# A transformer stack on one core: the order of loads, mask checks and value projections at the head of the first attention

## The chip, the core and the metric

The kernel is one program for one NeuronCore of a Trainium2 chip. TensorE (PE in the profile) multiplies matrices, VectorE (DVE), ScalarE (ACT) and GpSimd (POOL) do the rest, and SyncE (SP) issues most of the transfers. Each engine has a queue of its own, which it works off strictly in order; engines wait for each other by semaphores. The metric is the time of one execution on the device in microseconds (us).

## The reference, cut to what matters

Input are 2048 tokens `x` of width 256, a context of 1601 rows of width 256, and two integer masks of 2048 x 1601. Four layers follow, each a cross attention and a feed-forward block with a residual sum around each. Only the first attention and the masks matter here:

```python
x = x + L0_xattn(layernorm(x), ctx, Wq, Wk, Wv, Wo, bo)   # 8 heads of 64, no mask
# q = xn @ Wq, k = ctx @ Wk, v = ctx @ Wv, weights = (256, 512)
# out = softmax(q k^T / 8) v, then @ Wo + bo
```

The masks are used by later attentions only. The kernel has two versions of everything behind the first feed-forward block: a short one for masks of a certain pattern, and a general one. Which of them runs is decided by a look at all of both masks, and that look is done beside the first attention.

## The kernel before, in words

**Start.** `Net.__init__` issues 16 loads of `x`, one for each 128 tokens, on SP (L70). `load_context` issues 13 loads of context rows on ACT's queue (L123), transposes them on PE (L130) and copies the result into `ctxT` on ACT (L135). `attention0` then issues the four weights on SP (L313): keys, values, queries, output.

**Projections.** For each of four pairs of heads and four pieces of the context (512, 512, 512 and 65 columns) PE computes the keys (L338); ACT copies them in fp32 (`kT`, L342) and VectorE casts them to bf16 (`kb`, L343). Then PE computes the values for 13 tiles of context rows (L348), copied to `v` by VectorE for odd tiles (L353) and by ACT for even ones (L355). All these results pass through the same three PSUM banks (`pm`).

**Units.** The attention is worked in 16 units: 4 chunks of 512 tokens times 4 pairs of heads. `prepare` makes what a unit needs: the normalized tokens (once for each chunk), the queries (L367; copies L371 and L372), and the maximum of each row of scores. The maxima come from bf16 products, two heads side by side (L380), of which VectorE takes a maximum each (L385: 24 for each unit, then L396 and L400), and they are turned by PE (L406) into the shift `sh` (L407). The unit itself goes over 13 tiles of context rows, two tiles to a group `g`: `scores` (L458, L460 on PE, then the exponential on ACT, L465, into one of five buffers `p0`), and for the group before, `values` (L472 on PE; the sum of the exponentials on POOL, L479 and L481). Between these steps the generator of the next unit's `prepare` (`nxt`) and of the last unit's `finish` (`done`) are advanced by single steps. `finish` makes one product (L414), copies it (L418), takes four reciprocals on VectorE (L422) and multiplies (L424). Unit 0 has no predecessor, and so no `finish`; its own `prepare` runs ahead of it as a whole (L442).

**The looks at the masks.** `look_at_masks` is a generator. It loads 128 rows of a mask in two transfers, the first 1201 columns (`head`, L276) and the last 400 (`tail`, L278); ACT squares and adds up the head (L291), VectorE compares the tail with the first row of the mask (`mrow`, L293) and counts. There are 16 such looks for each mask, 32 in all, with two buffers. `attention0` advances the generator once at the end of unit 0 and then twice in each unit (L494).

**What sets the order.** In the first attention only PE's queue follows the source (L441, `manual_schedule`). The queues of ACT, VectorE, POOL and SP are ordered by a planner. It has put all 32 looks ahead of or into unit 0: on ACT the first comes behind four copies of keys, on VectorE the last one (L293, then L298 and L299) comes in the middle of unit 0.

Of the kernel before, what the change touches and what calls it, by code (L numbers as in the profile page):

```python
# [8 lines left out]
F32 = mybir.dt.float32  # L9
# [3 lines left out]
ALU = mybir.AluOpType  # L13
AX = mybir.AxisListType

P = 128
# [38 lines left out]
class Net:  # L55


    def __init__(self, ctx, tc, a, out):
        self.tc, self.nc, self.a, self.out = tc, tc.nc, a, out
        nc = self.nc  # L60
        self.const = ctx.enter_context(tc.tile_pool(name="const", bufs=1))
        self.small = ctx.enter_context(tc.tile_pool(name="small", bufs=4))
        self.wraw = ctx.enter_context(tc.tile_pool(name="wraw", bufs=3))
        self.xnp = ctx.enter_context(tc.tile_pool(name="xnp", bufs=2))


        self.x = []
        for t in range(NT):
            xt = self.const.tile([P, D], F32, name=f"x{t}")
            nc.sync.dma_start(xt, a["x"][0, t * P : (t + 1) * P, :])  # L70
            self.x.append(xt)

        self.ident = self.const.tile([P, P], F32, name="ident")
        make_identity(nc, self.ident)
        self.identb = self.const.tile([P, P], BF16, name="identb")
        make_identity(nc, self.identb)
        self.ones = self.const.tile([P, P], F32, name="ones")
        nc.vector.memset(self.ones, 1.0)
        self.negones = self.const.tile([1, P], BF16, name="negones")
        nc.vector.memset(self.negones, -1.0)  # L80
        self.mhalf = self.const.tile([P, TPC], F32, name="mhalf")
        nc.vector.memset(self.mhalf, -0.5)
        self.phalf = self.const.tile([P, TPC], F32, name="phalf")
        nc.vector.memset(self.phalf, 0.5)
        self.mone = self.const.tile([P, TPC], F32, name="mone")
        nc.vector.memset(self.mone, -1.0)

        self.ready = 0
        self.ctxT = self.const.tile([P, 2, NCTX], F32, name="ctxT")
# [161 lines left out]
    def look_at_masks(self, pool, names):  # L251

        nc = self.nc
        odd = pool.tile([P, len(names) * (2 * NT + 1)], F32, name="odd", bufs=1)
        self.rows = {}
        col = 0

        def flag():  # L260
            nonlocal col
            col += 1
            return odd[:, col - 1 : col]

        todo, loaded = [], []
        for k, n in enumerate(names):
            m = self.a[n].rearrange("b s k -> (b s) k") if n.startswith("mask_B") else self.a[n].rearrange("a b s k -> (a b s) k")
            row = self.const.tile([P, NTAIL], mybir.dt.int32, name=f"mrow{k}")
            nc.sync.dma_start(row, m[0, K0:].partition_broadcast(P))
            self.rows[n] = row  # L270
            todo += [(m, t, row) for t in range(NT)]

        def load():
            m, t, row = todo.pop(0)
            head = pool.tile([P, K0], mybir.dt.int32, name="head")
            nc.sync.dma_start(head, m[t * P : (t + 1) * P, :K0])  # L276
            tail = pool.tile([P, NTAIL], mybir.dt.int32, name="tail")
            nc.sync.dma_start(tail, m[t * P : (t + 1) * P, K0:])  # L278
            loaded.append((head, tail, row))

        for _ in range(2):
            load()
        yield
        for n in names:
            seen = self.small.tile([P, 1], F32, name="seen")
            junk = pool.tile([P, NTAIL], BF16, name="junk", bufs=1)
            nc.vector.tensor_scalar(junk, self.rows[n], 0.0, 0.0, ALU.not_equal, ALU.add, accum_out=seen)
            nc.vector.tensor_scalar(flag(), seen, 0.0, None, ALU.is_equal)
        while loaded:
            head, tail, row = loaded.pop(0)  # L290
            nc.scalar.activation(head, head, AF.Square, accum_out=flag())  # L291
            junk = pool.tile([P, NTAIL], BF16, name="junk", bufs=1)
            nc.vector.scalar_tensor_tensor(junk, tail, 1.0, row, ALU.mult, ALU.not_equal, accum_out=flag())  # L293
            if todo:
                load()
            yield
        self.some = self.const.tile([P, 1], F32, name="some")
        nc.vector.tensor_reduce(self.some, odd, AX.X, ALU.add)  # L298
        nc.vector.tensor_scalar(self.some, self.some, 0.0, None, ALU.is_gt)  # L299


    def attention0(self, look):

        tc, nc, a = self.tc, self.nc, self.a
        H, DH = 8, 64
        HP = H // 2
        halves = [slice(0, DH), slice(DH, P)]
        wk, wv = (x.rearrange("p (k f) -> p k f", k=2) for x in self.weights("kv0", 1024, 1024))
        wq, wo = self.weights("qo0", 1024, 1024)
        wq = wq.rearrange("p (k f) -> p k f", k=2)  # L310
        wo = wo.rearrange("p (k f) -> p k f", k=4)
        for v, n in ((wk, "Wk"), (wv, "Wv"), (wq, "Wq"), (wo, "Wo")):
            nc.sync.dma_start(v, a[f"L0_xattn_{n}"].rearrange("(k p) f -> p k f", p=P))  # L313
        with ExitStack() as s:
            self.banks(s, m=3, a=1)
            kv = s.enter_context(tc.tile_pool(name="kv0", bufs=1))
# [17 lines left out]
            for hp in range(HP):  # L334
                for k0, n in PIECES:
# [5 lines left out]
                        )  # L341
                    nc.scalar.copy(kT[:, hp, k0 : k0 + n], ps[:, :n])  # L342
                    nc.vector.tensor_copy(kb[:, hp, k0 : k0 + n], ps[:, :n])  # L343
            for kt in range(NKT):
                r = rows_of(kt)
                ps = self.pm()
                for kc in range(2):
                    nc.tensor.matmul(  # L348
                        ps[:r, :], lhsT=self.ctxT[:, kc, kt * P : kt * P + r], rhs=wv[:, kc, :],
                        start=kc == 0, stop=kc == 1,  # L350
                    )
                if kt % 2:
                    nc.vector.tensor_copy(v[:r, kt, :], ps[:r, :])  # L353
                else:
                    nc.scalar.copy(v[:r, kt, :], ps[:r, :])  # L355

            xnTs = {}

            def prepare(c, hp, made):
# [78 lines left out]

            units = [(c, hp) for c in range(NCH) for hp in range(HP)]
            made = []  # L440
            s.enter_context(tc.manual_schedule(engines={mybir.EngineType.PE}))  # L441
            drain(prepare(*units[0], made))  # L442
            attn = done = None
            for u, (c, hp) in enumerate(units):
                nxt = prepare(*units[u + 1], made) if u + 1 < len(units) else None
# [39 lines left out]
                for g, kts in enumerate(groups):  # L485
# [5 lines left out]
                    for kt in late:  # L491
                        values(kt)
                    late = kts
                    if u and g in (3, 5):  # L494
                        step(look, 1)
                    if g:
                        step(nxt, 1)
# [1655 lines left out]
@with_exitstack  # L2153
def network(ctx: ExitStack, tc: tile.TileContext, a, out):
    net = Net(ctx, tc, a, out)
    net.load_context()
    masks = ("mask_BxSxS2_ik0", "mask_1x1xSxS2_ik0")
    with tc.tile_pool(name="look", bufs=2) as pool:
        net.attention0(net.look_at_masks(pool, masks))
    room = ctx.enter_context(tc.tile_pool(name="w1", bufs=1)).tile([P, 1536], F32, name="w1")  # L2160
    dram = ctx.enter_context(tc.tile_pool(name="e0d", bufs=1, space=bass.MemoryType.DRAM))
    odd, due, gates, raw = net.experts0(dram, ("L1_xattn", room))
# [67 lines left out]
```

## Time and profile before

| | |
|---|---|
| median of 3 runs | 1833.39 us (1827.76 to 1833.9) |
| the profiled execution | 1826.28 us, its span 1824.2 us |
| granted clock of TensorE, mean | 0.976 |
| PE busy | 1699.6 us of the span |
| first product of keys (L338) | at 19.97 us |
| first product of values (L348) | at 46.14 us |
| first scores of unit 0 (L458) | at 95.72 us |
| end of unit 0 (copy L505) | at 144.10 us |
| end of unit 1 (copy L505) | at 179.36 us |
| looks, head on ACT (L291) | 1.21 us each, and 0.19 us for reading the sum |
| looks, tail on VectorE (L293) | 0.56 to 2.59 us, median 0.58 us |

The profile covers one execution. Each digit of a row of engines is the busy share of 1/40 of the span in tenths, so each slice is 45.6 us. A line of the timeline gives the start, the time, the engine and the source line of a group of instructions, and in brackets how long the engine had been idle and what ended that. A line of the chain of waits gives start, time and what the end of the program had to wait for there. In a table of stretches, the columns after the time are the busy times of PE, the weight loads, VectorE, ACT and POOL with the number of instructions, then the granted clock, the busy share of the transfer engines, and GB/s.

### The profile page before, as it was taken

Reading aid. Unit: us, or ns where it says so; the run is one execution under the profiler, and the core shown is the slowest. Engines: PE = TensorE matmul, PEld = TensorE weight load, DVE = VectorE, ACT = ScalarE, POOL = GpSimd, SP = SyncE. Lnnn points to the kernel's source line nnn. Section 1 sums busy time; section 2 is a strip of 40 time slices with the busy share of each in tenths; the row PEclk is TensorE's granted clock in tenths of the full one; section 3 lists DMA queues with packets and bytes.
Section 4 is the critical chain, followed back from the end, with each engine's and each line's share of the span. In section 5 each row is a group of like instructions: output and inputs, shape, how many; then the busy total and the mean of one; then the engine's idle time right before and its main releaser. Section 6 shows DMA issues by size and latency. Waiting matters only on the chain.

```text
span 1824.2 us, 21267 instructions
## 1 busy us (share of the span) xinstructions
PE 1699.6 (93%) x8102; PEld 848.0 (46%) x8102; DVE 909.8 (50%) x1737; ACT 728.5 (40%) x963; POOL 690.8 (38%) x477
## 2 busy tenths in 40 slices
PE   6879999999999998999999999999988789999898
PEld 3323334333333334444457863664576622332687
DVE  4664565555664543662844643422045567786300
ACT  3554443453443442223234522111135456666222
POOL 2047886876887683002202730100026400211210
PEclk9889999999999998999999999999989889999999
DMA  8870000000000000454300010000000001010651
GB/s 271 280 229 1 1 1 1 1 1 1 1 1 1 1 0 12 163 220 173 111 13 1 1 32 1 1 1 0 0 1 1 13 13 21 17 22 13 221 184 39
DMA packets 52461, 94.11 MB, mean 52 GB/s; under 512 B 10093, under 2 KB 37374, under 8 KB 51454
## 3 DMA queue, kind: packets, MB, share of 16 engines
q1 hardware_dynamic: 49776, 88.92, 14.8%
q0 software_dynamic: 768, 2.10, 0.4%
q10 hardware_dynamic: 1806, 1.64, 0.3%
q8 instruction: 66, 1.08, 0.2%
q14 instruction: 45, 0.37, 0.1%
HBM read 69.30 MB, written 19.01 MB: 48 GB/s over the span
## 4 chain that ended last, share of the span: by engine, by line
PE 72%; DVE 12%; ACT 5%; DMA 4%; POOL 3%; issue 3%; SPq 0%; ACTq 0%; DVEq 0%; POOLq 0%
PE pa L472 8%; PE psc L460 6%; PE pa L557 6%; PE psc L1058 5%; PE pa L1078 5%; PE psc L1980 4%; DVE mp L385 4%; PE pa L2143 3%; PE psc L2132 3%; DVE ri L422 3%; PE pa L1449 2%; PE psc L458 2%; ACT p L1987 2%; PE pm L380 2%; PE pm L431 2%
## 5 line engine op out<-in xcount | busy, mean ns | idle before, releaser
L481 POOL TENSOR_TENSOR sp<-sp,p 128x1024 f32<-128x1024 f32 (+1 forms) x176 | 418.5, 2378 | 57.7 <-ACT p L465 47.0
L385 DVE TENSOR_REDUCE mp<-pm 128x1 f32<-128x512 f32 x384 | 242.8, 680 | 159.7 <-PE pm L380 159.0
L465 ACT ACTIVATE p<-psc 128x1024 f32<-128x1024 f32 (+1 forms) x208 | 212.9, 1024 | 260.5 <-PE psc L460 166.9
L460 PE MATMUL psc<-qT,kT 64*128 64x512 f32 (+1 forms) x832 | 221.6, 594 | 0.0
L472 PE MATMUL pa<-p,v 128*64 128x512 f32 (+1 forms) x832 | 202.3, 608 | 0.0
L1987 ACT ACTIVATE p<-psc 100x1024 f32<-100x1024 f32 x128 | 124.4, 1021 | 62.7 <-PE psc L1980 54.7
L1965 DVE TENSOR_REDUCE ms<-psc 128x2 bf16<-128x800 f32 x128 | 124.2, 988 | 46.0 <-PE psc L1961 43.4
L380 PE MATMUL pm<-kb,qb 64*128 64x512 bf16 x384 | 100.5, 389 | 27.5 <-DVE mp L385 26.0
L557 PE MATMUL pa<-w_e,xe 128*128 128x512 f32 x256 | 118.7, 614 | 0.0
L472 PEld LDWEIGHTS pa<-p,v 128*64 128x64 f32 (+1 forms) x832 | 50.9, 137 | 129.8 <-issue 126.8
L1058 PE MATMUL psc<-q,kT 128*128 128x512 f32 (+1 forms) x208 | 102.2, 610 | 0.0
L171 DVE TENSOR_SCALAR xn<-x,mv,rstd 128x256 f32<-128x256 f32 x128 | 58.2, 512 | 87.7 <-PE pm L185 52.2
L156 POOL TENSOR_SCALAR rstd<-mv 128x4 f32<-128x4 f32 x32 | 9.8, 308 | 228.6 <-DVE mv L152 185.2
L1078 PE MATMUL pa<-v,p 128*128 128x257 f32 (+1 forms) x416 | 95.3, 382 | 0.0
L460 PEld LDWEIGHTS psc<-qT,kT 64*128 64x128 f32 (+1 forms) x832 | 86.0, 185 | 19.5 <-issue 6.3
L1980 PE MATMUL psc<-q,kT 32*100 32x512 f32 x512 | 82.0, 653 | 13.2 <-ACT p L1987 11.5
L458 PE MATMUL psc<-sh,negz 64*128 64x512 bf16 (+1 forms) x416 | 87.7, 384 | 2.1 <-ACT sh L407 2.0
L1030 DVE TENSOR_REDUCE mp<-pm 128x1 f32<-128x512 f32 x64 | 34.4, 571 | 102.5 <-PE pm L1025 102.2
L1078 PEld LDWEIGHTS pa<-v,p 128*128 128x128 f32 (+1 forms) x416 | 77.5, 190 | 11.8 <-issue 0.2
L567 ACT COPY y<-pa 128x512 f32<-128x512 f32 x64 | 37.6, 587 | 96.6 <-PE pa L557 94.3
L557 PEld LDWEIGHTS pa<-w_e,xe 128*128 128x128 f32 x256 | 48.0, 194 | 55.6 <-issue 52.3
L479 POOL TENSOR_TENSOR sp<-p,p 128x1024 f32<-128x1024 f32 x16 | 37.7, 2354 | 89.4 <-ACT p L465 89.4
(376 smaller groups left out, 2730.2 us busy)
## 6 DMA issues: line engine op xcount, KB each, us to landing
table<-y SPq DMA_DIRECT2D x32, 512.0 KB, 3.2
w<-in_L_ffn_w_dram SPq DMA_DIRECT2D x16, 1024.0 KB, 6.2
head<-in_mask_BxSxS_ik_dram SPq DMA_DIRECT2D x16, 600.5 KB, 4.0
head<-in_mask_1x1xSxS_ik_dram SPq DMA_DIRECT2D x16, 600.5 KB, 4.0
bc<-turned SPq DMA_DIRECT2D x7, 1024.0 KB, 7.0
tail<-in_mask_BxSxS_ik_dram SPq DMA_DIRECT2D x16, 200.0 KB, 4.1
tail<-in_mask_1x1xSxS_ik_dram SPq DMA_DIRECT2D x16, 200.0 KB, 3.6
x<-in_x_dram SPq DMA_DIRECT2D x16, 128.0 KB, 4.0
```

What stands on the lines that cost most here:

```text
L380: nc.tensor.matmul(pair[j][:, :wd], lhsT=qb[h, i * P : (i + 1) * P], rhs=kb[h, hp, k0 : k0 + wd], start=True, stop=True,)
L385: nc.vector.tensor_reduce(mp[:, i, j, n : n + 1], pair[j][:, :wd], AX.X, ALU.max)
L460: nc.tensor.matmul(sc[:r, j, :], lhsT=kT[h, hp, kt * P : kt * P + r], rhs=q[h, :], start=False, stop=True,)
L465: nc.scalar.activation(p[:r], sc[:r], AF.Exp, scale=DH**-0.5)
L472: nc.tensor.matmul(acc[h, :], lhsT=v[:r, kt, hp * P + h.start : hp * P + h.stop], rhs=p[:r, j, :], start=kt == 0, stop=kt == NKT - 1,)
L481: nc.gpsimd.tensor_tensor(sums[:r], sums[:r], p[:r], ALU.add)
L557: nc.tensor.matmul(ps, lhsT=xnT[t // TPC][:, kc, (t % TPC) * P : (t % TPC + 1) * P], rhs=ew[kc][:, 2 * h : 2 * h + 2, :], start=kc == 0, s ...
L1058: nc.tensor.matmul(sc[:r, j, :], lhsT=kT[:, kc, ks], rhs=q[:, kc, :], start=kc == 0, stop=False)
L1078: nc.tensor.matmul(acc[:, : D + 1], lhsT=p[:r, kt, i * P : (i + 1) * P], rhs=v[:r, kt, :], start=kt == 0, stop=kt == NKT - 1,)
L1965: nc.vector.tensor_reduce(ms[u % 2][:, i, 64 * k + DH : 64 * k + 64 : 32], ps[:, :, :NTAIL], AX.X, ALU.max)
L1980: nc.tensor.matmul(sc[j // 2][:TR, j % 2, :], lhsT=kT[h, g, kt * TR : (kt + 1) * TR], rhs=q[u][h, :], start=True, stop=True,)
L1987: nc.scalar.activation(p[:TR], sc[k][:TR], AF.Exp, scale=DH**-0.5)
```

## The change

1. The weights of the keys are issued ahead of everything else on SP (`weights0`), then those of the values; the 16 loads of `x` come behind these two, and then the weights of queries and outputs.
2. A look loads its 1601 columns in one transfer, `both`; head and tail are views of it.
3. In the first attention ACT's queue follows the source too. Each look makes ACT copy one element per partition (`one`, from a tile of ones) behind its pass over the head, and VectorE's pass over the tail takes `one` as its factor in place of the constant 1.0, so it can't start before ACT's.
4. The generator of the looks is advanced three times in a unit, in groups 1, 3 and 5, instead of twice.
5. The 13 products of values are made between the steps of the first unit's `prepare`, instead of ahead of it.

In the generated order of after, VectorE's and SP's queues are still the planner's. All 32 looks then stand in units 1 to 11. In VectorE's queue of such a unit, the first look stands behind 4 of the 24 maxima; the second behind `finish`'s multiplication and 4 more maxima; the third behind the last maxima. Two small passes over the masks' first rows (L287, L288 of before) stay between the second and third cast of keys, and the statistics of all 16 tiles of `x` (L151) stay ahead of the first cast. Apart from looks, the queues of units 1 to 15 and of all that follows hold the same instructions in the same order.

```diff
         self.x = []
         for t in range(NT):
-            xt = self.const.tile([P, D], F32, name=f"x{t}")
-            nc.sync.dma_start(xt, a["x"][0, t * P : (t + 1) * P, :])
-            self.x.append(xt)
+            self.x.append(self.const.tile([P, D], F32, name=f"x{t}"))
...
         def load():
             m, t, row = todo.pop(0)
-            head = pool.tile([P, K0], mybir.dt.int32, name="head")
-            nc.sync.dma_start(head, m[t * P : (t + 1) * P, :K0])
-            tail = pool.tile([P, NTAIL], mybir.dt.int32, name="tail")
-            nc.sync.dma_start(tail, m[t * P : (t + 1) * P, K0:])
-            loaded.append((head, tail, row))
+            both = pool.tile([P, NCTX], mybir.dt.int32, name="both")
+            nc.sync.dma_start(both, m[t * P : (t + 1) * P, :])
+            loaded.append((both[:, :K0], both[:, K0:], row))
...
             nc.scalar.activation(head, head, AF.Square, accum_out=flag())
+
+            one = self.small.tile([P, 1], F32, name="one")
+            nc.scalar.copy(one, self.ones[:, 0:1])
             junk = pool.tile([P, NTAIL], BF16, name="junk", bufs=1)
-            nc.vector.scalar_tensor_tensor(junk, tail, 1.0, row, ALU.mult, ALU.not_equal, accum_out=flag())
+            nc.vector.scalar_tensor_tensor(junk, tail, one, row, ALU.mult, ALU.not_equal, accum_out=flag())
...
-    def attention0(self, look):
+    def weights0(self):
+        wkv = self.weights("kv0", 1024, 1024)
+        self.nc.sync.dma_start(
+            wkv[0].rearrange("p (k f) -> p k f", k=2), self.a["L0_xattn_Wk"].rearrange("(k p) f -> p k f", p=P)
+        )
+        return wkv
+
+    def attention0(self, look, wkv):
...
-        for v, n in ((wk, "Wk"), (wv, "Wv"), (wq, "Wq"), (wo, "Wo")):
+        for v, n in ((wv, "Wv"), (wq, "Wq"), (wo, "Wo")):
             nc.sync.dma_start(v, a[f"L0_xattn_{n}"].rearrange("(k p) f -> p k f", p=P))
+            if n == "Wv":
+                for t in range(NT):
+                    nc.sync.dma_start(self.x[t], a["x"][0, t * P : (t + 1) * P, :])
...
-            for kt in range(NKT):
...
-                    nc.scalar.copy(v[:r, kt, :], ps[:r, :])
...
-            s.enter_context(tc.manual_schedule(engines={mybir.EngineType.PE}))
-            drain(prepare(*units[0], made))
+            s.enter_context(tc.manual_schedule(engines={mybir.EngineType.PE, mybir.EngineType.Activation}))
+
+            first = prepare(*units[0], made)
+            for kt in range(NKT):
+                r = rows_of(kt)
+                ps = self.pm()
+                for kc in range(2):
+                    nc.tensor.matmul(
+                        ps[:r, :], lhsT=self.ctxT[:, kc, kt * P : kt * P + r], rhs=wv[:, kc, :],
+                        start=kc == 0, stop=kc == 1,
+                    )
+                if kt % 2:
+                    nc.vector.tensor_copy(v[:r, kt, :], ps[:r, :])
+                else:
+                    nc.scalar.copy(v[:r, kt, :], ps[:r, :])
+                if kt:
+                    step(first, 2 if kt > 1 else 1)
+            drain(first)
...
-                    if u and g in (3, 5):
+                    if u and g in (1, 3, 5):
                         step(look, 1)
...
     net = Net(ctx, tc, a, out)
+    wkv = net.weights0()
     net.load_context()
...
-        net.attention0(net.look_at_masks(pool, masks))
+        net.attention0(net.look_at_masks(pool, masks), wkv)
```

More of the change, by code (lines that the diff above doesn't have):

```diff
@@ L307, in attention0 @@
         halves = [slice(0, DH), slice(DH, P)]
-        wk, wv = (x.rearrange("p (k f) -> p k f", k=2) for x in self.weights("kv0", 1024, 1024))
+        wk, wv = (x.rearrange("p (k f) -> p k f", k=2) for x in wkv)
         wq, wo = self.weights("qo0", 1024, 1024)
@@ L343, in attention0 @@
                     nc.vector.tensor_copy(kb[:, hp, k0 : k0 + n], ps[:, :n])
-            for kt in range(NKT):
[L345 to L354, printed above, removed]
-                    nc.scalar.copy(v[:r, kt, :], ps[:r, :])
             xnTs = {}
```

## The prediction

> **What bounds the kernel now.** First the page, for the share of each engine and where in the span PE isn't full:
>
> ```profile
> PE 1699.6 (93%) x8102; PEld 848.0 (46%) x8102; DVE 909.8 (50%) x1737; ACT 728.5 (40%) x963; POOL 690.8 (38%) x477
> PE   6879999999999998999999999999988789999898
> DMA  8870000000000000454300010000000001010651
> ```
>
> PE is the bound, except in the first three slices (137 us), where the transfers are full. Then those slices stage by stage, in the table of stretches:
>
> ```profile
> 46.00:70.00 24.00, 22.84 (x56) 9.79 (x56) 9.18 (x24) 14.08 (x24) 0.00 (x0) 1.00 0.82 267
> 70.00:96.00 26.00, 16.74 (x51) 5.01 (x51) 20.45 (x41) 14.45 (x24) 3.31 (x4) 0.69 0.84 288
> 96.00:144.00 48.00, 39.47 (x172) 14.27 (x172) 30.06 (x57) 27.15 (x36) 27.55 (x12) 0.88 0.60 190
> 144.00:179.40 35.40, 34.12 (x178) 11.95 (x178) 19.87 (x32) 16.07 (x19) 28.55 (x13) 1.00 0.00 1
> ```
>
> Unit 0 (third row) takes 48 us, unit 1 only 35.4. What unit 0 waits for is in the chain of waits: mask transfers, each released by the look before it.
>
> ```profile
> 85.91 1.30 ACT head L291 x2
> 87.23 4.03 DMA head<-in_mask_1x1xSxS_ik_dram
> ...
> 115.83 3.52 DMA tail<-in_mask_1x1xSxS_ik_dram
> 119.44 2.21 DVE junk L293 x2
> ```
>
> Last the looks themselves, by tile, and then the timeline, POOL beside VectorE:
>
> ```profile
> L293 DVE SCALAR_TENSOR_TENSOR junk<-tail,mrow x32: 557/576/2591, 30.7 to 127.7; 128x400 bf16<-128x400 int32 x32
> ```
>
> ```profile
> 110.02 2.45 POOL L481 TENSOR_TENSOR sp<-sp,p 128x1024 f32<-128x1024 f32 x1 [0.18 <-ACT p L465]
> 118.86 5.00 POOL L481 TENSOR_TENSOR sp<-sp,p 128x1024 f32<-128x1024 f32 x2 [6.38 <-ACT p L465]
> 110.32 2.59 DVE L293 SCALAR_TENSOR_TENSOR junk<-tail,mrow 128x400 bf16<-128x400 int32 x1
> 119.44 2.21 DVE L293 SCALAR_TENSOR_TENSOR junk<-tail,mrow 128x400 bf16<-128x400 int32 x1 [0.62 <-DMA tail<-in_mask_1x1xSxS_ik_dram]
> ```
>
> The same look takes 0.56 us or four times that: the first slow one ends at 112.91, 0.44 after POOL's sum (110.02 + 2.45 = 112.47). The second gets in between two sums. Every slow look ends about 0.44 us behind a POOL sum.
>
> **The change, part by part.** It takes the looks out of the head and puts three into each of units 1 to 11. So two sums.
>
> *Keys.* L338 starts at 19.97, waiting for Wk, the 17th load on SP. Now Wk is first, 16 loads of `x` come later by two transfers, and the first normalization isn't needed before 45 us: hidden. ACT must first issue its 13 context loads (until 12.6) and load its table (1.28), so PE can start at 12.5 to 15. But VectorE's queue is next: 16 statistics, two casts, the two passes over `mrow`, then the other casts. The last statistic ended at 17.9; 1 MB of weights now goes ahead of `x`, at 0.27 MB/us 3.7 us: 21.5. Two casts: 23. `mrow` has the same bytes ahead of it on SP as before, so it lands as before: 18.31 + 7.3 = 25.6. Two passes (1.35): the third cast starts at 27.0, against 30.0. PE can run only three banks ahead; at 27.6 it has 8 large pieces (4 records of 0.43 = 1.72) and 3 small ones (0.22) left, 14.4: end 42.0, against 46.1. Bounds of this gain: 0 (`mrow` 4 us later) and 7.5 (no wait but PE's).
>
> *Values and the first maxima.* Before: 46.1 to 95.7, 49.6 us, of which PE's 52 records of values are 22.4 and VectorE's 24 maxima are 14.4 (16 took 9.55 from 80.5 on, 0.60 each), one after the other, with ACT's waits for masks between, and at half clock from 80 to 100. Now: three products of values, 8 transposes (1.0) and the queries (1.7): 7.9. Then six rounds of one product (1.72) and four maxima. The next product needs the bank of the second maximum, 1.6 us after the last product's end where ACT copies it, 2.0 where VectorE does: 6 x 3.55 = 21.3. Then four products, the last maxima and the turn: 8.3. Sum 37.5. Bounds: PE alone 28.5; nothing overlapped 43.5.
>
> *Unit 0.* 48.4 before. Unit 1's 35.3 less `finish`'s product (1.1) and PE's waits for the reciprocals (1.8): 32.4; PE alone 31.2, all of unit 1 35.3.
>
> End of unit 0: 42.0 + 37.5 + 32.4 = 111.9 against 144.1, gain 32. One stretch at half clock after the wait near 25 would cost 1.7: I take 31, from 25 to 36.
>
> *Looks in a steady unit.* ACT: 1.21 + 0.19 + the one-column copy, not in the trace; nearest is the reading of the sum, 0.19. Together 1.5 (the reading overlaps). It fits before the next exponential at all three places (gaps of 2.47, 2.97 and 2.04 us in unit 1), so ACT costs nothing; without that gap 1.6 each. Transfers: one of 0.8 MB in place of two is issued two looks, some 20 us, ahead, in units where nothing else is moved: nothing (a landing took 3.6 to 6.2). SP issues 32 instead of 64; past its first two mask loads go the two expert weights of 1 MB, the second waiting for the buffer of keys' and values' weights; the third mask load behind it isn't needed before unit 1. VectorE, by unit 1's timeline:
>
> ```profile
> 151.98 9.63 POOL L481 TENSOR_TENSOR sp<-sp,p 128x1024 f32<-128x1024 f32 x4
> 153.21 2.58 DVE L385 TENSOR_REDUCE mp<-pm 128x1 f32<-128x512 f32 x4 [0.92 <-PE pm L380]
> 162.26 5.05 POOL L481 TENSOR_TENSOR sp<-sp,p 128x1024 f32<-128x1024 f32 x2 [0.64 <-ACT p L465]
> 165.93 3.87 DVE L385 TENSOR_REDUCE mp<-pm 128x1 f32<-128x512 f32 x6 [0.86 <-PE pm L380]
> ```
>
> Look A (group 1) comes behind the exponential that ends at 151.88; with ACT's 1.5 and a semaphore it is released at 153.5, in the middle of a sum that ends at 151.98 + 2.41 = 154.4 (9.63 for four); with 0.44 and the reading (0.08) it ends at 154.95. The maxima behind it start 1.7 us late. Behind those are queued the bank for L414, its copy, the reciprocals, the multiplication and the next maxima, and PE waits for all of them in turn (the chain of waits runs over them from 153.2 to 163.3 in this unit). PE's maximum of 154.08 waits for a bank till 155.6, L414 moves from 154.64 to 156.2: PE loses 1.55. Look B (group 3), behind the exponential that ends at 164.1, is released at 165.7; the second of the two sums ends at 167.3, the look at 167.8; the maxima that started at 165.93 are 1.9 late, PE's next maximum needs a bank and PE loses 1.6. Look C finds VectorE idle: nothing. So 3.15 a unit, and 32 looks are 11 units: 34.7.
>
> *A rule against the change.* The rows say that a look beside a sum ends after it. The Trainium skill's "SBUF — State Buffer", section "Who interferes with whom", has it as a rule: a VectorE instruction with two inputs in SBUF and a GpSimd one that reads SBUF exclude each other for the whole instruction, and the first to start keeps the port. A look reads tail and `mrow`; a sum reads two tiles. By the median row (0.58) A would cost 0.9 and B 0.1, 11 us in all; by row and rule, 35. POOL is busy 28.55 of unit 1's 35.40 us, against 27.55 of 48 in unit 0, so the median there isn't the price here. I take 35, between 11 and 45.
>
> *Sum.* -31 + 35 = +4. The profiled execution's 1826.28 (its span 1824.2 and 2.1 around it) becomes 1830; the shown median is 7.1 above that execution, so 1833.4 + 4 = **1837**. Before and after can't be told apart within 0.5% (9.2 us).
>
> **Rivals.**
>
> *Break-even* (0.48): as above, 1837, by itself 1826 to 1843. Speaks for it: both sums rest on rows of units. Against: they are differences of large terms.
>
> *The looks don't find the sums* (0.20): they cost 11 us, 31 are gained: 1833.4 - 20 = 1813. For: positions within a unit can shift by a few tenths, and a look that meets the end of a sum pays almost nothing. Against: the sums follow each other without a gap at both places.
>
> *Half clock in the units* (0.14), slower: A and B make PE idle for about 1.5 us in one piece. The granted clock fell to 0.50 behind stretches of 3.41 us in which PE was busy 1.67, 1.01 and 1.53 us, and not behind those with 1.79 and more (but for one of 2.20). "TensorE: Matmul & The Clock Gate" (Part 1) tells of an idle window; these rows say that a half-idle one is enough. By the page's rule no unit drops; by the rows the case decides itself at 1.7 busy, and A and B leave about 1.8 to 2.1. If half of the 22 places fall below it, each at 1.7 us (half of 3.4), 19 are lost: 1856.
>
> *A poor head* (0.15): `mrow` late and the rounds of values waiting longer, gain 20 instead of 31: 1848. For: VectorE's queue still holds statistics and `mrow` ahead of the casts. Against: rounds have no wait for a transfer.
>
> *A look loses the port to the next sum as well* (0.03): A would wait till 161.6, 7 us a unit: 1910. One row (119.44) speaks against.
>
> That the looks move back to the head can't be: VectorE's wait for ACT's copies, and ACT follows the source.
>
> **Numbers.** Likeliest 1837. The range takes in break-even, the poor head and half each of the first and third rival, 0.80: 1812 to 1856. Faster 0.20 (looks that miss the sums), same 0.48, slower 0.32.
>
> **What the profile after would show.** Right: L338 before 15 us, but the third cast of keys near 27; values from 42; unit 0 ending at 112; units 1 to 11 near 38.4 us and 12 to 15 near 35.3; looks A and B of 0.6 to 2.5 us, ending 0.44 behind a sum. Wrong: units of 36 us with looks of 0.56 (second case), clock under 1.00 in units 1 to 11 (third), or unit 0 ending behind 120 (fourth).

## The result, and the profile after

| | before | after |
|---|---|---|
| median of 20 runs | 1829.22 us (1821.85 to 1833.9) | 1836.14 us (1831.11 to 1838.72) |
| ratio | | 1.0037, 95% interval 1.0026 to 1.0049 |
| profiled execution, its span | 1826.28, 1824.2 us | 1838.18, 1836.5 us |
| first product of keys | 19.97 | 14.27 |
| first product of values | 46.14 | 44.38 |
| first scores of unit 0 | 95.72 | 83.75 |
| end of unit 0 | 144.10 | 115.88 |
| end of unit 11 | 551.67 | 557.54 |
| end of unit 15 | 693.55 | 699.42 |

The change gains 28.2 us up to the end of unit 0 and loses 34.1 in units 1 to 11. At the end of the first attention it is 5.9 us behind, and the medians say 6.9.

The page of after, the shares and the slices:

```profile
PE 1704.1 (93%) x8102; PEld 849.6 (46%) x8102; DVE 936.0 (51%) x1737; ACT 729.6 (40%) x995; POOL 694.7 (38%) x477
PE   6898999999899998999999989999988789999899
DMA  6002121111110000364300010000000000010651
```

The transfers are dense in the first slice alone now, at six tenths. The masks are spread over slices 4 to 12, and VectorE is busy for 26 us more than before with the same 32 looks. The stages of after in the table of stretches (keys, values, unit 0, unit 2, unit 13; after the time: busy PE, weight loads, VectorE, ACT, POOL, granted clock, share of the transfers, GB/s):

```profile
14.27:44.38 30.11, 27.01 (x79) 13.51 (x79) 14.95 (x46) 9.52 (x21) 6.55 (x10) 0.94 0.55 175
44.38:83.75 39.37, 34.18 (x103) 12.37 (x103) 22.59 (x39) 6.66 (x13) 2.98 (x4) 1.00 0.00 0
83.75:115.88 32.13, 32.13 (x173) 11.28 (x174) 16.32 (x27) 15.40 (x17) 25.85 (x11) 1.00 0.10 34
154.23:192.58 38.35, 34.73 (x176) 12.00 (x176) 24.01 (x38) 19.82 (x28) 29.12 (x13) 1.00 0.20 64
600.82:636.08 35.26, 33.98 (x176) 11.81 (x176) 19.87 (x32) 16.03 (x19) 27.55 (x12) 1.00 0.00 1
```

Unit 0 is a stage of PE alone: 32.13 us busy of 32.13. Units 2 and 13 hold the same 176 records of PE; with three looks the unit takes 3.09 us more. Those looks, by tile, and then in the timeline of unit 2, with what stands around the first two:

```profile
L292 DVE SCALAR_TENSOR_TENSOR junk<-both,one,mrow x32: 634/1593/2786, 125.0 to 541.4; 128x400 bf16<-128x400 int32 x32
```

```profile
162.11 7.41 POOL L493 TENSOR_TENSOR sp<-sp,p 128x1024 f32<-128x1024 f32 x3
163.31 1.59 DVE L292 SCALAR_TENSOR_TENSOR junk<-both,one,mrow 128x400 bf16<-128x400 int32 x1 [0.90 <-ACT one L290]
164.83 2.47 DVE L381 TENSOR_REDUCE mp<-pm 128x1 f32<-128x512 f32 x4
165.56 0.37 PE L376 MATMUL pm<-kb,qb 64*128 64x512 bf16 x1 [0.97 <-DVE mp L381]
...
173.87 5.07 POOL L493 TENSOR_TENSOR sp<-sp,p 128x1024 f32<-128x1024 f32 x2 [1.74 <-ACT p L477]
177.01 2.35 DVE L292 SCALAR_TENSOR_TENSOR junk<-both,one,mrow 128x400 bf16<-128x400 int32 x1 [0.34 <-ACT one L290]
179.30 3.07 DVE L381 TENSOR_REDUCE mp<-pm 128x1 f32<-128x512 f32 x5
180.03 0.37 PE L376 MATMUL pm<-kb,qb 64*128 64x512 bf16 x1 [1.24 <-DVE mp L381]
```

The median look has gone from 0.58 to 1.59 us. Of the three sums that start at 162.11, the first two stand alone in the timeline as

```profile
162.11 2.35 POOL L493 TENSOR_TENSOR sp<-sp,p 128x1024 f32<-128x1024 f32 x1
164.54 2.56 POOL L493 TENSOR_TENSOR sp<-sp,p 128x1024 f32<-128x1024 f32 x1
```

The first ends at 164.46, and look A at 164.90. The two from 173.87 end at 178.94, look B at 179.36. Both looks end some 0.43 behind a sum; the maxima are next on VectorE, and PE waits 0.97 and 1.24 us for a bank of theirs.

The head, from the timeline:

```profile
21.48 0.69 DVE L352 CAST kb<-pm 128x512 bf16<-128x512 f32 x1 [0.74 <-ACT kT L351]
25.71 0.57 DVE L283 TENSOR_SCALAR_CACHE_REDUCE junk<-mrow 128x400 bf16<-128x400 int32 x1 [3.54 <-DMA mrow<-in_mask_BxSxS_ik_dram]
...
27.06 1.41 DVE L352 CAST kb<-pm 128x512 bf16<-128x512 f32 x3
27.80 16.75 PE L347 MATMUL pm<-ctxT,w_kv 128*128 128x512 f32 x44 [3.10 <-DVE kb L352]
```

VectorE stands before `mrow` for 3.54 us, PE then waits 3.10 us for the third cast, and from 27.36 to 30.77 its clock is 0.50.

### The profile page after: what moved, and what is told of

Read it like the earlier page. It is cut to its first block, busy times and chain, and to the rows that moved or that the text cites. A ratio compares the mean times of both kernels' runs of the same rounds, so it can differ in the third digit from the quotient of the medians.

```text
span 1836.5 us, 21240 instructions
## 1 busy us (share of the span) xinstructions
PE 1704.1 (93%) x8102; PEld 849.6 (46%) x8102; DVE 936.0 (51%) x1737; ACT 729.6 (40%) x995; POOL 694.7 (38%) x477
## 4 chain that ended last, share of the span: by engine, by line
PE 70%; DVE 13%; ACT 6%; issue 5%; POOL 3%; DMA 1%; SPq 1%; ACTq 0%; DVEq 0%; POOLq 0%
PE psc L472 6%; PE pa L484 6%; PE psc L1070 5%; PE pa L569 5%; PE pa L1090 5%; PE psc L1992 4%; DVE mp L381 3%; PE psc L2144 3%; PE pa L2155 3%; DVE ri L418 3%; DVE junk L292 2%; ACT p L1999 2%; PE psc L470 2%; PE pm L427 2%; PE pm L363 2%
## 5 line engine op out<-in xcount | busy, mean ns | idle before, releaser
L493 POOL TENSOR_TENSOR sp<-sp,p 128x1024 f32<-128x1024 f32 (+1 forms) x176 | 423.1, 2404 | 76.3 <-ACT p L477 67.8
L1977 DVE TENSOR_REDUCE ms<-psc 128x2 bf16<-128x800 f32 x128 | 124.3, 989 | 47.0 <-PE psc L1973 44.5
L470 PEld LDWEIGHTS <-negz 64*128 64x128 bf16 (+1 forms) x416 | 21.6, 94 | 113.2 <-issue 113.0
```

Source lines behind the costliest of these rows:

```text
L470: nc.tensor.matmul(sc[:r, j, :], lhsT=negz[h, :r], rhs=sh[h, :], start=True, stop=False)
L493: nc.gpsimd.tensor_tensor(sums[:r], sums[:r], p[:r], ALU.add)
L1977: nc.vector.tensor_reduce(ms[u % 2][:, i, 64 * k + DH : 64 * k + 64 : 32], ps[:, :, :NTAIL], AX.X, ALU.max)
```

## The experiments

My theory: looks A and B are held by POOL's running sums, since both read two tiles in SBUF, and what they cost is what is queued behind them on VectorE. One rival is ScalarE's part: its work on a look in source order, or VectorE's wait for its copy. Another is that a look in a unit simply costs its time, wherever it stands. For the head: is its gain in the order of the loads, in the interleaving, or in the looks that left?

The clearest measure is where units end, since a unit of the same queues repeats within 0.02 us from kernel to kernel as long as the clock stays. All kernels but e5, whose units differ by design (us; whole: the median; e2, e4, e6, e7, e8, e11 and e12 were timed once, and the medians of the kernel before, timed beside the kernels of the table, lay between 1826.18 and 1828.25):

| kernel | end of unit 0 | unit 2 alone | end of unit 11 | end of unit 15 | whole |
|---|---|---|---|---|---|
| before | 144.10 | 35.26 | 551.67 | 693.55 | 1829.22 |
| after | 115.88 | 38.35 | 557.54 | 699.42 | 1836.14 |
| e1_one_input | 115.55 | 35.79 | 528.99 | 670.85 | 1804.56 |
| e2_no_act_wait | 116.23 | 39.85 | 573.45 | 715.33 | 1856.55 |
| e3_late_looks | 115.94 | 37.81 | 558.28 | 700.16 | 1833.70 |
| e4_no_looks | 115.23 | 35.26 | 522.80 | 664.68 | 1798.64 |
| e6_values_alone | 120.53 | 38.35 | 562.22 | 704.09 | 1840.62 |
| e7_x_first | 117.13 | 38.36 | 557.57 | 699.45 | 1832.68 |
| e8_rows_later | 111.36 | 38.34 | 551.21 | 693.08 | 1826.68 |
| e9_both | 111.27 | 37.82 | 553.00 | 694.87 | 1831.18 |
| e10_two_late | 110.51 | 35.27 | 518.12 | 660.00 | 1799.36 |
| e11_looks_only | 123.45 | 38.34 | 564.74 | 706.62 | 1840.09 |
| e12_act_free | 143.19 | 35.27 | 548.85 | 690.73 | 1827.98 |

### What a look costs

**e1: one tile instead of two.**

```diff
-            nc.vector.scalar_tensor_tensor(junk, tail, one, row, ALU.mult, ALU.not_equal, accum_out=flag())
+            nc.vector.tensor_scalar(junk, tail, one, 0.0, ALU.is_gt, ALU.add, accum_out=flag())
```

> The 32 looks keep their place and their wait for ScalarE's one-column copy, but read one tile in SBUF instead of two (tail alone; the comparison with the first row is left out, the instruction only counts entries above the copied 1). POOL theory (a look is held by POOL's running sum because both read two tiles in SBUF): no look longer than about 0.7 us, look A ends 0.9 us earlier and look B 1.6, units 1 to 11 fall from 38.35 us to about 36.2 (35.9 to 36.5), the whole by 22 to 26 us to about 1812. ScalarE theory (the looks are late because VectorE waits for ScalarE's copy in source order): the wait is the same, so the units stay at 38.3 and the whole at 1836. More-looks theory (each look costs its own 0.6 us of VectorE and that is all): the units can't have lost 3.1 us to looks of 0.6, so nothing changes either.

The looks of this kernel by tile:

```profile
L292 DVE TENSOR_SCALAR_CACHE_REDUCE junk<-both,one x32: 614/629/632, 124.6 to 514.6; 128x400 bf16<-128x400 int32 x32
```

No look takes more than 0.632 us, in the same place, behind the same wait. The unit falls to 35.79 (a little below the expected 35.9 to 36.5), and the whole to 1804.56 against 1826.18 of the kernel before on the same chip (ratio 0.9879, 0.9852 to 0.9905). So the second tile in SBUF makes 2.56 of the 3.09 us of a unit. The other 0.53 is lost at look A. The four maxima behind it, first in unit 2 of the kernel before (which starts at 179.36), then here (from 151.33):

```profile
188.47 2.58 DVE L385 TENSOR_REDUCE mp<-pm 128x1 f32<-128x512 f32 x4 [0.92 <-PE pm L380]
160.97 2.48 DVE L381 TENSOR_REDUCE mp<-pm 128x1 f32<-128x512 f32 x4
```

They start 9.64 us into the unit instead of 9.11, and from the next product on all of PE runs 0.53 later; look B adds nothing. ScalarE's pass isn't in the way, since the exponential behind it starts 10.26 into the unit in both kernels. But VectorE stood 0.90 us before the look for ScalarE's copy, so the 0.53 is as much this wait's as the look's.

This is the reading of the Trainium skill's "SBUF — State Buffer" ("Who interferes with whom"): a VectorE instruction with two inputs in SBUF contends with a GpSimd instruction that reads SBUF, and one with a single input, outside the two-port modes, does not. The traces show it in the other direction too. In after, 17 sums start while a look still has 0.35 to 0.54 us to run, and take 2.55 to 2.76 us instead of 2.35 (the second row above in unit 2); here ten sums start so, and take 2.34 to 2.37.

**e4: no looks.** The squares, copies and comparisons are taken out of the generator's loop.

```diff
             head, tail, row = loaded.pop(0)
-            nc.scalar.activation(head, head, AF.Square, accum_out=flag())
-
-            one = self.small.tile([P, 1], F32, name="one")
-            nc.scalar.copy(one, self.ones[:, 0:1])
-            junk = pool.tile([P, NTAIL], BF16, name="junk", bufs=1)
-            nc.vector.scalar_tensor_tensor(junk, tail, one, row, ALU.mult, ALU.not_equal, accum_out=flag())
             if todo:
                 load()
...
-        nc.vector.tensor_reduce(self.some, odd, AX.X, ALU.add)
+        nc.vector.tensor_reduce(self.some, odd[:, :2], AX.X, ALU.add)
```

> The squares, the one-column copies and the comparisons of all 32 looks are left out (the loads of the masks and the two passes over the first rows stay). All theories in which the looks cost the 34 us: units 1 to 11 take 35.3 us like units 12 to 15, end of unit 11 at 523 instead of 557.5, whole about 1802. If the mask transfers or SP's issues have a share in the loss, the units stay above 35.3 by that share.

Unit 2 takes 35.26, unit 11 ends at 522.80, the whole is 1798.64. The mask transfers and SP's issues, which stay, cost the units nothing.

**e5: the places one by one.**

```diff
-                    if u and g in (1, 3, 5):
+                    if u and g == (1, 3, 5)[(u-1) // 5]:
```

> One look a unit, in group 1 in units 1 to 5, in group 3 in units 6 to 10, in group 5 in units 11 to 15; the 17 looks that remain follow behind the last unit, so the whole is longer by some 40 to 60 us and isn't compared. POOL theory with the prediction's terms: +1.5 us a unit in units 1 to 5, +1.6 in units 6 to 10, 0 in units 11 to 15 (over 35.3 us). More-looks and ScalarE theories: the same for every place, about +1.0 a unit.

Measured from end to end of a unit: 36.73 to 36.74 in units 1, 2 and 5 (look A), 36.86 to 36.87 in units 6, 9 and 10 (look B), 36.53 in unit 11 (look C), where the kernel before has 36.52. Units 12 to 15, with a look C each, take what they take in the kernel before. So A costs 1.48, B 1.61 and C nothing; A and B make 3.09, the whole loss of unit 2. Units 4 and 8, in which a chunk is finished, pay the same 1.48 and 1.60; only in unit 3, which prepares a new chunk, A costs 0.57. That the price depends on the place by so much, and is nothing for C, speaks against a price of the look as such.

**e2: VectorE doesn't wait for ScalarE.**

```diff
-            nc.vector.scalar_tensor_tensor(junk, tail, one, row, ALU.mult, ALU.not_equal, accum_out=flag())
+            nc.vector.scalar_tensor_tensor(junk, tail, 1.0, row, ALU.mult, ALU.not_equal, accum_out=flag())
```

> The looks take their factor 1.0 as an immediate instead of ScalarE's copy, so VectorE doesn't wait for ScalarE; ScalarE keeps its order and its copies. Three looks a unit still, the first now behind eight maxima and ahead of the reciprocals, the second behind eight more, the third behind the last reduction; two looks move into the keys. POOL theory: they are held by sums as before, and what is queued behind the first two still waits: units between 36.3 and 38.8, looks up to 2.8 us. ScalarE theory: without the wait the loss goes, units 35.3 to 35.6.

Both were wrong: unit 2 takes 39.85 us, units 1 and 3 take 41.40 and 40.37. The looks still take up to 2.58 us, so it isn't the copied factor that makes them long. What VectorE was idle for ahead of the looks:

```profile
  DMA both<-in_mask_1x1xSxS_ik_dram: 53.3, 16
  DMA both<-in_mask_BxSxS_ik_dram: 38.1, 15
```

With nothing but their own data to wait for, the planner puts looks into VectorE's queue ahead of the landing of their mask, whose load is issued only when ScalarE, in source order, has squared an earlier one. VectorE then stands before the transfer for 91.4 us in all, 2.9 each. In after a look waits 31.0 us in all for `one`, and never for a mask. So the loss doesn't go with the wait for ScalarE; in after this wait is what keeps the looks behind the landing of their masks.

### Where a look costs nothing

**e3: later places.**

```diff
-                    if u and g in (1, 3, 5):
+                    if u and g in (4, 5, 6):
```

> The three looks of a unit stand in groups 4, 5 and 6 instead of 1, 3 and 5; nothing is left out. POOL theory: the looks may still be held by sums, up to 2.8 us each, but only the last maxima of the next unit stand behind the first of them and nothing behind the others, so units 1 to 11 take 35.3 to 35.8 us and the whole falls by 28 to 34 us to 1802 to 1808, faster than the kernel before (1829). ScalarE theory (its squares of 1.2 us in source order delay the exponentials) and more-looks theory: three looks a unit cost what they cost wherever they stand, units 38.3, whole 1836.

A miss: 1833.70 us, ratio 1.0040 (1.0022 to 1.0059); units 1, 2, 5, 6 and 10 take 37.82 or 39.45. Unit 2 in the timeline:

```profile
181.99 2.78 DVE L292 SCALAR_TENSOR_TENSOR junk<-both,one,mrow 128x400 bf16<-128x400 int32 x1 [0.89 <-ACT one L290]
184.69 1.28 DVE L381 TENSOR_REDUCE mp<-pm 128x1 f32<-128x512 f32 x2
185.43 0.28 PE L387 MATMUL pm<-kb,qb 64*128 64x65 bf16 x7 [2.36 <-DVE mp L381]
...
189.20 1.63 DVE L292 SCALAR_TENSOR_TENSOR junk<-both,one,mrow 128x400 bf16<-128x400 int32 x1 [2.34 <-ACT one L290]
...
192.75 1.17 DVE L292 SCALAR_TENSOR_TENSOR junk<-both,one,mrow 128x400 bf16<-128x400 int32 x1 [1.91 <-ACT one L290]
```

The look of group 4 still stands ahead of the last two large maxima, and PE needs the banks of these for the short products (L387): 2.36 us of waiting, all of the unit's 2.56 but 0.2. The looks of groups 5 and 6 are held too (1.63 and 1.17), and nobody waits for them. So I had missed two instructions behind the look. Unit 9 is the check on it: there the look of group 4 starts at 470.29, shortly ahead of the end of a sum, and takes 0.65 us; PE waits 0.24, and the unit takes 35.67. The units of 39.45 are those in which this wait falls wholly into one 3.41-us stretch of the grid to which the drops of the clock keep (last section); the table of stretches has the one ahead of the drop in unit 1 and the drop itself:

```profile
143.57:146.98 3.41, 1.04 (x16) 0.50 (x12) 3.41 (x6) 1.02 (x1) 3.33 (x2) 1.00 0.22 45
146.98:150.40 3.42, 3.42 (x10) 0.77 (x8) 0.84 (x3) 2.29 (x4) 2.12 (x2) 0.50 0.48 195
```

PE was busy for 1.04 us of the first, and the second ran at half clock: 39.45 - 37.82 = 1.63, half of 3.41 but for 0.07.

**e10: two late looks,** in groups 5 and 6 alone, and four in the last unit, which prepares nothing. It also has the edit of e8 (below).

```diff
-                    if u and g in (1, 3, 5):
+                    if u and g in ((5, 6) if nxt else (3, 4, 5, 6)):
```

> After the late looks: the look in group 4 held the banks of the last maxima for 2.4 us, those in groups 5 and 6 held nothing. So two looks a unit, in groups 5 and 6 (in the last unit four, groups 3 to 6), and the passes over mrow behind ScalarE's copy; nothing is left out. If the price of a look is only what is queued behind it on VectorE, all units take what they take without looks (35.26, 36.5, 43.27), end of unit 0 at 111.3, the whole at 1793 to 1799, ratio to the kernel before about 0.982. If POOL's lock costs in every place because POOL itself falls behind and frees the exponentials' buffers late, units 36 to 38, whole 1810 to 1830.

1799.36 us against 1828.25 (ratio 0.9833, 0.9803 to 0.9863), a shade above the expected 1793 to 1799: 1.7% faster than the kernel before, with nothing left out. Against e8, from which it differs by the places alone, the places are worth 33.1 us at the end of unit 11. The units take 35.26, 36.5 and 43.27 as without looks. Unit 2 of this kernel in the table of stretches:

```profile
145.77:181.04 35.27, 34.00 (x176) 11.81 (x176) 22.62 (x37) 18.56 (x25) 28.74 (x13) 1.00 0.20 69
```

And its looks by tile:

```profile
L296 DVE SCALAR_TENSOR_TENSOR junk<-both,one,mrow x32: 633/1475/2631, 142.1 to 659.7; 128x400 bf16<-128x400 int32 x32
```

They are still long (median 1.48, up to 2.63), so sums hold them as in after. The price was not the length of a look as such but the maxima that stand behind it. ScalarE's squares aren't in the way here either.

### The head

**e6: values alone,** ahead of the preparation.

```diff
-                if kt:
-                    step(first, 2 if kt > 1 else 1)
             drain(first)
```

> The values' projections stand ahead of the first unit's preparation again instead of between its maxima; all else as in the changed kernel. If the interleaving carries the gain of this stage, the stage from the first value product to the first score of unit 0 grows from 39.4 us to about 43.5 (products 22.4, transposes and queries 2.7, 24 maxima at 0.60 and the turn), or 45 to 47 with one or two stretches at half clock beside the maxima; end of unit 0 at 120 to 124 instead of 115.9. If the overlap is worth nothing, because each product waits for the bank of a maximum, it stays at 39.4.

From the first product of values (42.09) to the first scores (86.60) it takes 44.5 us instead of 39.4, as expected. Unit 0 then takes 33.9 instead of 32.1, since its start still ran at half clock (17.1 us from 73.3 on, beside the maxima alone). So the interleaving is worth 6.9 us here. Up to the values the two kernels have the same queues, but here `mrow` landed 0.8 us sooner; from the timeline:

```profile
24.88 0.57 DVE L283 TENSOR_SCALAR_CACHE_REDUCE junk<-mrow 128x400 bf16<-128x400 int32 x1 [2.13 <-DMA mrow<-in_mask_BxSxS_ik_dram]
26.97 15.29 PE L347 MATMUL pm<-ctxT,w_kv 128*128 128x512 f32 x44 [1.69 <-DVE kb L352]
42.09 4.08 PE L444 MATMUL pm<-w_kv,ctxT 128*128 128x512 f32 x9
```

PE's wait was 1.69 us instead of 3.10, no half clock followed, and the keys ended at 42.09 instead of 44.38.

**e7: x first.** The 16 loads of `x` go back to where they are created, ahead of the keys' weights.

```diff
-            self.x.append(self.const.tile([P, D], F32, name=f"x{t}"))
+            xt = self.const.tile([P, D], F32, name=f"x{t}")
+            nc.sync.dma_start(xt, a["x"][0, t * P : (t + 1) * P, :])
+            self.x.append(xt)
...
-            if n == "Wv":
-                for t in range(NT):
-                    nc.sync.dma_start(self.x[t], a["x"][0, t * P : (t + 1) * P, :])
```

> The 16 loads of x stand ahead of the keys' weights on SP again; all else as in the changed kernel. If the third cast of the keys is held by the two passes over mrow until 27.06 whatever precedes it, an earlier first product is worth nothing: first key product near 20 instead of 14.3, third cast still near 27, keys end 44.4 within 1.0, end of unit 0 near 115.9. If the keys' weights first carried the gain of the head, the keys end 3 to 6 us later, end of unit 0 at 119 to 122.

The first product of keys is at 19.73, the third cast at 29.51 (not near 27), the keys end at 45.64 and unit 0 at 117.13. The two expectations had left a gap, and the result lies in it. Keys' weights first is worth 1.25 us as it stands, because what it gains is spent on the wait for `mrow` and the half clock behind it; against the 42.09 of e6, where that stretch is missing, it is 3.6. Neither is sharp: after, e1, e3, e4, e5 and e6 have the same queues up to the values, and their keys end between 42.09 and 44.44, the passes over `mrow` starting between 24.63 and 25.71.

**e8: the passes over `mrow` later.**

```diff
+        zeros = pool.tile([P, 1], F32, name="zeros", bufs=1)
+        nc.gpsimd.memset(zeros, 0.0)
...
-            nc.vector.tensor_scalar(junk, self.rows[n], 0.0, 0.0, ALU.not_equal, ALU.add, accum_out=seen)
+            zero = self.small.tile([P, 1], F32, name="zero")
+            nc.scalar.copy(zero, zeros)
+            nc.vector.tensor_scalar(junk, self.rows[n], zero, 0.0, ALU.not_equal, ALU.add, accum_out=seen)
```

> The two passes over mrow take their zero from a copy that ScalarE makes in unit 1, so they stand behind it in VectorE's queue and not between the second and third cast of the keys. If mrow's landing and these passes hold the keys, the third cast starts near 23 instead of 27.06, the wait of TensorE of 3.1 us at 27.8 and the half clock behind it go, the keys end at 38.5 to 39.5 instead of 44.4, unit 0 ends near 111; unit 1 gets 0.6 to 2 us longer; sum -3 to -5. If the casts themselves or TensorE bound the keys, the end of the keys moves by less than 1.5.

The casts and PE in the timeline:

```profile
21.18 1.29 DVE L356 CAST kb<-pm 128x512 bf16<-128x512 f32 x2
23.50 0.83 DVE L356 CAST kb<-pm 128x512 bf16<-128x512 f32 x2 [1.02 <-ACT kT L355]
39.87 3.65 PE L448 MATMUL pm<-w_kv,ctxT 128*128 128x512 f32 x8
```

The third cast starts at 23.50, PE doesn't wait, no half clock follows, and the keys end at 39.87 (38.5 to 39.5 expected): 4.5 us earlier, as is the end of unit 0 (111.36). Unit 1 isn't longer, as expected, but 0.56 us shorter. The two passes and one of the four maxima more than fill the 0.89 us in which VectorE had waited for ScalarE's copy, and the look behind them starts so near the end of the sum that had held it that it takes 0.63 us instead of 1.59.

**e9: e8 and the places of e3 together.**

> The passes over mrow behind ScalarE's copy in unit 1, and the looks in groups 4, 5 and 6. The two gains add up, since they lie in different stretches: 28 to 34 from the looks and 3 to 5 from the keys, 1836 to 1797 to 1805, ratio to the kernel before 0.983 to 0.987. If the late looks collide with the end of a unit (the turn of the maxima stands behind them), less than half of it: 1818 to 1822.

The first part is there (unit 0 ends at 111.27), the second isn't: from unit 2 on 37.82 a unit as in e3, with five stretches at half clock in the units. 1831.18 us, ratio 1.0017 (1.0006 to 1.0028), beyond both of the expected ranges. This is what put the weight on group 4 alone, and e10 followed from it.

**e11: only the looks leave the head.** The edits of e6 and e7 together.

> Both other parts of the change undone: loads of x first, values alone ahead of the preparation; what stays is ScalarE's source order with the looks behind it. If the head's parts add up (1.25 for the order of loads, 4.65 for the interleaving, measured one by one), unit 0 ends at 121 to 123 and the looks leaving the head are worth about 22 of the 28 us. If the parts need each other (no gain of one without the others), it ends behind 130.

Unit 0 ends at 123.45, just past the expected 121 to 123. So of 28.2 us, 20.65 come from the looks leaving the head and 7.57 from the other two parts, which one by one had shown 1.25 and 4.65. The looks leave because ScalarE follows the source, and no run separates these two; nor was the single transfer of a look tried alone.

**e12: ScalarE not held to the source.**

```diff
-            s.enter_context(tc.manual_schedule(engines={mybir.EngineType.PE, mybir.EngineType.Activation}))
+            s.enter_context(tc.manual_schedule(engines={mybir.EngineType.PE}))
```

> ScalarE isn't held to the source's order; all else as in the changed kernel. Its squares and copies then come as early as masks land, all looks within the keys, the values and unit 0, as in the kernel before. Looks-in-the-head theory: units 1 to 11 take 35.3, unit 0 ends some 15 to 28 us later than 115.9 (131 to 144), the whole at 1815 to 1830. If the looks cost nothing beside interleaved values: unit 0 still ends near 117 and the whole is about 1803.

All looks are back in the head (28.6 to 142.0), and unit 0 ends at 143.19, 0.91 ahead of the kernel before. This mark is late here, since the last look stands ahead of the copy on ScalarE:

```profile
141.98 1.21 ACT L287 ACTIVATE both<-both 128x1201 int32<-128x1201 int32 x1 [1.44 <-DMA both<-in_mask_1x1xSxS_ik_dram]
143.19 0.57 ACT L517 COPY o<-pa 128x512 f32<-128x512 f32 x1
```

PE begins unit 1 at 141.14 instead of 143.99, and at the end of unit 11 the lead is 2.8. So keys' weights first and the interleaving, worth 7.57 us when the looks have left, are worth some 2.8 when they haven't (with the single transfer, which e12 keeps). The waits of this kernel from 20 to 143 us (in total, times, longest) say what the head waits for:

```profile
DVE junk L292 <- DMA both<-in_mask_1x1xSxS_ik_dram: 15.3, 11, 2.3
ACT both L287 <- DMA both<-in_mask_1x1xSxS_ik_dram: 12.9, 12, 2.1
ACT both L287 <- DMA both<-in_mask_BxSxS_ik_dram: 12.4, 11, 2.3
DVE junk L292 <- DMA both<-in_mask_BxSxS_ik_dram: 9.1, 4, 3.5
```

ScalarE and VectorE stand in turn before masks, at a look every 3.5 us (32 in 113.4). That what PE does sooner then waits behind the next mask fits this, but no run shows it by itself.

## Why the prediction was right

*Looks.* 3.15 us a unit was predicted from the timeline of a unit without looks, 3.09 measured; A 1.55 and 1.48, B 1.60 and 1.61, C nothing. Over units 1 to 11 34.7 and 34.1. Two things cancel in this: units 3 and 7, which prepare a new chunk, lost only 2.2 each (look A costs less there, 0.57 in e5), and unit 11, which prepares one too and has a stretch at half clock from 529.12 to 532.53, lost 5.1. The choice of row and rule (35) over the median row (11) was what decided the sign of the whole, and e1 shows that choice right by its cause. One slow look of before, 1.06 us at 73.59, ended behind another POOL instruction with two tiles in SBUF (L435), so it is not sums alone that hold a look.

*Keys.* The first product at 14.27 (12.5 to 15) and the third cast at 27.06 (27.0) are there. The end is 44.38 and not 42.0: that is the half-clock stretch, which the text had named at 1.7 and which cost 2.3 together with the later landing, as e6 without it ends at 42.09.

*Values and first maxima.* 39.4 and not 37.5. The mis-sized term is the round: from product to product they took 3.86, 3.68, 3.96, 3.69, 3.96 and 3.68, together 22.8, where 6 x 3.55 = 21.3 had been counted. The timeline of PE has both of its terms longer:

```profile
56.22 1.98 PE L444 MATMUL pm<-w_kv,ctxT 128*128 128x512 f32 x4 [0.23 <-DVE mp L381]
58.13 0.39 PE L376 MATMUL pm<-kb,qb 64*128 64x512 bf16 x2
59.90 1.98 PE L444 MATMUL pm<-w_kv,ctxT 128*128 128x512 f32 x4 [0.23 <-DVE mp L381]
```

A product occupies PE for 1.91 us, not 1.72, and the next one follows its end by 1.77, not 1.6, where ScalarE copies (2.04 for 2.0 where VectorE does). The stage's first part (8.0 for 7.9) and last part (8.6 for 8.3) held. Two terms of the prediction are off by hundredths, by their own working (3.55 should be 3.52, the end of look A 154.92), and change nothing.

*Unit 0.* 32.1 for 32.4. Together: end at 115.88 instead of 111.9, gain 28.2 instead of 31.

*The sum.* +5.9 at the end of the attention instead of +4. That the predicted 1837 meets the measured 1836.14 so closely owes something to chance: the three runs shown had a median 4.2 above that of twenty (1829.22), and the sum was 2.9 too small against the medians' 6.9. Twenty executions of each kernel do tell the two apart, though they differ by less than the 0.5% that the text had thought necessary.

*Rivals.* "The looks don't find the sums": fell, the median look is 1.59. "A look loses the port to the next sum too": fell, each gets in between two sums. "Half clock in the units": one stretch in 22 places (behind 1.50 us busy at 525.71), the other places had 2.12 or more. Its point of decision, 1.7 us busy, holds for the stalls of 2.4 us in e3, which leave 1.04 to 1.41 busy where the clock drops. But it isn't sharp: the reading left out two stretches of before, behind which the clock stayed full, and in e6 the clock dropped behind 2.05. "A poor head": partly, by the round and the stretch, 28 where it had 20. The two stretches of before that the reading left out:

```profile
69.84:73.26 3.42, 1.67 (x10) 1.09 (x9) 2.32 (x6) 2.83 (x6) 1.33 (x2) 1.00 0.86 261
121.04:124.45 3.41, 1.47 (x8) 0.78 (x8) 3.41 (x7) 1.64 (x4) 2.72 (x2) 1.00 0.95 294
```

What the prediction didn't see: that the parts of the head don't add up (e11, e12), and what follows from its own finding that the third place is free: e10, which gives up the first two places, is 1.5% faster than e8.

## What to carry to other kernels

An instruction that another engine's long stream can hold, as POOL's sums hold a look here, costs what stands behind it in its own queue, so list that before moving it, down to the short ones (e3 failed on two maxima), and put it where nothing is behind it (e10). A wait that looks like a burden may be what holds a planner to a sensible place (e2), and a small pass that waits for a transfer must not stand between the copies that free banks (e8). Measure the parts of a change in both orders: two of them were worth 7.6 us or some 2.8, depending on whether the third was there (e12).

## What the runs showed of the hardware that I had not expected

Behind the first attention, executions of the same instructions differ by where their half-clock stretches fall. From the end of unit 15 to the end of the span, in the table of stretches, before:

```profile
693.55:1824.20 1130.65, 1058.92 (x5052) 609.03 (x5052) 530.38 (x1051) 413.13 (x573) 217.58 (x247) 0.97 0.16 51
```

and after:

```profile
699.42:1836.50 1137.08, 1066.78 (x5052) 613.88 (x5052) 531.11 (x1051) 413.19 (x573) 217.29 (x247) 0.97 0.16 51
```

The same 5052 records of PE are busy for 7.9 us more. In this part the clock was at 0.50 for 61 us in before and for 79 in after, and it took 1130.6 us in e3 (66 us at 0.50) and 1139.0 in e9 (82). So 6.4 us of the 12.3 between the two profiled spans are not likely to be the change's: the medians of twenty differ by 6.9, of which 5.9 stand at the end of unit 15.

That the drop is a matter of phase too is seen in the units of e3: the same wait of 2.36 us costs 2.56 or 4.19, depending on how it lies to a grid of 3.41 us (in before the drops begin at 80.08, 107.38 and 114.21, 8 and 2 times 3.41 apart). The Trainium skill's "TensorE: Matmul & The Clock Gate" (Part 1) tells of an idle window of about that length; here 1.04 us busy out of 3.41 was idle enough, and in after 1.50, while 1.47 in before was not.
